# Spare products in TensorE's early pauses, a last result stored in three pieces, and new due times for the first groups of a planned graph-network kernel

## The chip, the core and the metric

The kernel runs on one core of a Trainium2 chip. The metric is the device time of one execution, in microseconds (us). Three runs of the kernel before gave 1441.22, 1442.35 and 1445.91; the median is 1442.35. Engines are called PE (TensorE), DVE (VectorE), ACT (ScalarE), POOL (GpSimd) and SP (SyncE, which here issues nearly all DMAs).

## What is computed

128 graphs of 64 nodes with 256 features pass through four residual layers. Each layer takes a layernorm and a relu of the running x and adds its result to x:

```python
h = jnp.maximum(_layernorm(x), 0.0); x = x + _L0_gnn_ref(h, adj, ...)   # attention, 4 heads of 64, elu
h = jnp.maximum(_layernorm(x), 0.0); x = x + _L1_gnn_ref(h, adj, ...)   # attention, 1 head of 256, elu
h = jnp.maximum(_layernorm(x), 0.0); x = x + _L2_gnn_ref(h, nodemask, adj, ...)  # relations by label, relu
h = jnp.maximum(_layernorm(x), 0.0); x = x + _L3_gnn_ref(h, adj, ...)   # three GRU steps
...
for i in range(3):                       # inside _L3_gnn_ref
    m = h @ weight[i]
    aggr = jnp.einsum('bst,bsd->btd', A, m)
    h = _gru_cell(aggr, h, w_ih, w_hh, b_ih, b_hh)
```

Everything is float32. The adjacency holds only zeros and ones, so of layer 2 only the relation with label 1 has edges. The kernel computes that case in its planned part and holds a general part behind a flag, which these inputs do not take.

## The kernel before, in words

**Tiling.** Two graphs fill 128 partitions; four such pairs are a group (`G = 4`, `T = 512` columns), and there are 16 groups. Each group goes through layers 0, 1 and 2 (`first_layer`, `second_layer`, `third_layer`), then through `before` (layernorm of the GRU's input and its first product along the edges) and `recur`, the three GRU steps. Groups 0 and 1 are split into two units of two pairs, `(p0, n) = (0, 2)` and `(2, 2)`; the second unit of group 0 uses tiles of its own (names ending in `e`, as `t0e`, `hT1e`, `u2e`), so that its work can lie beside that of the first. From group 2 on a group is one unit. Groups 0 and 1 transpose on PE (`layernorm_T`), later ones by 32x32 blocks on DVE and 16 DMAs (`layernorm_T_by_dma`).

**Setting up.** Beside groups 0 and 1 the kernel prepares weights: the columns of the attention vectors (`attention_columns`, on DVE), the loop relation's weights `wl`, and the GRU's weights `wc` and `whh` (`later_weights`, mostly PE products copied out by ACT).

**What orders the work.** The code does not run in program order. Each operation is noted with an estimated cost (`Plan.note`, function `cost`), and `Plan.emit` then acts as a list scheduler: it keeps one planned clock for each engine (`free`), finds for each engine the ready operation that can start first, settles ties by a due time, and emits it. A result is planned to reach another engine `LATENCY` (160.9 ns) after its end. The due times come from jobs opened by `nc.begin(name, start, end, after)`: an operation's due time lies between the job's start and end according to the work still behind it. The stretches of each unit's three layers are the tuples `at` in `units`; from group 3 on they are `end - 55.6 * i`. `start` (99.2) and `period` (83.2) give the due times of the recurrences. The engines then run these fixed orders and wait on semaphores; the plan's times themselves bind nothing on the chip.

**PSUM.** Eight banks: three tagged `mt`, shared by products of all layers, and five owned by the recurrence (`ry`, `rm`, `rz`, `nh`, `ni`). Until the recurrence first takes one of its own, the others may borrow all five (`Banks.place`, `early`).

**The end.** The recurrence works on the features in two chunks of 128. After the last step `back` transposes a chunk on PE and DVE adds the residual x out of PSUM into `hnat`: chunk 0 in the middle of the last step, chunk 1 after it. Then one DMA stores all of `hnat` (512 KB). After that each engine reads the flag and branches past the general part.

In the profile all planned operations carry the line of `emit` (L380) and the packed products of `beside` carry L601, so names of tiles are used here: `hn`, `hT` are a layernorm and its transpose, `t` the attention weights, `u` and `v` layer 2, `st`, `mv`, `var` the layernorm's statistics, `tp` a PSUM bank with transposes, `mm` one with products.

Of the kernel before, what the change touches and what calls it, by code (L numbers as in the profile page):

```python
# [20 lines left out]
G = 4  # L21
# [186 lines left out]
class Plan:  # L208

    LATENCY = 160.9

    def __init__(self, nc):
        self.nc, self.on, self.ops, self.job = nc, False, [], None
        self.jobs = {}
        for name in ENGINES:
            setattr(self, name, Engine(self, name))

# [46 lines left out]
    def emit(self):  # L266
# [45 lines left out]
        while left:  # L312
            best = None
            for e, ops in ready.items():
                found = None
                for op in ops:
                    t = max(free[e], op.ready)
                    if best is not None and t > best[0] or found is not None and t > found[0] and t > free[e]:
                        continue
                    if any(j.left for j in op.job.after):  # L320
                        continue
                    places = {}
                    for b in op.needs:
                        if b.real is None:
                            taken = [tag for x, tag in places.items() if x.pool is b.pool]
                            tag = b.pool.place(b, taken)
                            if tag is None:
                                break
                            places[b] = tag
                            t = max(t, b.pool.released(tag, b, taken.count(tag)))  # L330
                    else:
                        key = (t, op.due)
                        if found is None or key < found[:2]:
                            found = (*key, op, places)
                if found is not None and (best is None or found[:2] < best[:2]):
                    best = found
            assert best is not None, "nothing can be emitted"
            t, _, op, places = best
            e = op.engine
            ready[e].remove(op)  # L340
            for b, tag in places.items():
                b.pool.put(b, tag)
            op.call()
            op.start = t
            if op.dma:
                free[e] = t + 665.0
                wire = max(wire, t + 1350.0) + op.cost
                op.end = wire + 400.0
            else:
                took = op.cost  # L350
                if op.port:
                    other = "Pool" if e == "DVE" else "DVE"
                    took = max(took, held[other] + min(op.port, took) - t)
                    held[e] = t + took
                op.end = t + took + (165.0 if e == "PE" else 0.0)
                free[e] = t + took - min(early.get(e, 0.0), op.cost / 2)
            for b in op.bases:
                b.left -= 1
                b.end = max(b.end, op.end)
            op.job.left -= 1  # L360
            left -= 1
            for other in op.then:
                other.waits -= 1
                if not other.waits:
                    enter(other)
# [71 lines left out]
def kernel(  # L437
# [167 lines left out]
        writes = list({id(x[0].base): x[0] for x in products}.values())  # L605
        nc.note("PE", emit, cost, [Plan.all_of(x) for x in writes], [x for p in products for x in p[1:]])

    def elu_add(work, src, o, engine):

        em = work.tile(list(o.shape), F32, name="em")  # L610
        nc.vector.tensor_scalar(em, o, 0.0, None, op0=ALU.min)
        nc.scalar.activation(em, em, AF.Exp)
        nc.vector.scalar_tensor_tensor(em, em, -1.0, o, op0=ALU.add, op1=ALU.max)
        engine.tensor_tensor(src, src, em, ALU.add)

# [3 lines left out]
            b = slice(half * N, (half + 1) * N)  # L619
            nc.vector.tensor_scalar(dst[b, :, b], src[b], scalar, None, op0=op)  # L620

    def values(work, psum, src, heads, we, by_dma=False, graphs=False):


        fo = D // heads
        n = src.shape[1]
        hT = work.tile([P, K, n * P], F32, name="hT")
        if by_dma:
            layernorm_T_by_dma(work, src, hT, graphs=graphs)
        else:  # L630
            layernorm_T(work, psum, src, hT, graphs=graphs)
        wh = work.tile([P, n, D + heads], F32, name="wh")
        wv = wh.rearrange("p g (h f) -> p g h f", h=heads)
        nc.gpsimd.memset(wv[:, :, :, fo:], 1.0)
        es = work.tile([P, n, 2 * heads], F32, name="es")
        for p in range(n):
            pm = psum.tile([P, 512], F32, name="mm")
            for k in range(K):
                nc.tensor.matmul(
                    pm[:, : D + 2 * heads], pair(hT, k, p) if graphs else hT[:, k, p * P : (p + 1) * P], we[:, k, :],  # L640
                    start=(k == 0), stop=(k == K - 1),
                )
            nc.scalar.copy(wv[:, p, :, :fo], pm[:, :D].rearrange("p (h f) -> p h f", h=heads))
            nc.vector.tensor_copy(es[:, p, :], pm[:, D : D + 2 * heads])
        return wv, es

    def aggregate(work, psum, lhsT, wv, heads):
# [13 lines left out]
            )  # L661
        return o.rearrange("p g h f -> p g (h f)")

    def aggregate_graphs(work, psum, t, wv, heads):


        fo = D // heads
# [2 lines left out]
        for u in range(n // 2):  # L670
# [9 lines left out]
            for r in range(2):  # L680
                rec = work.tile([P, heads], F32, name="rec")
                nc.vector.reciprocal(rec, pv[r][:, :, fo])
                nc.vector.tensor_tensor(
                    o[:, 2 * u + r], pv[r][:, :, :fo], rec[:, :, None].to_broadcast([P, heads, fo]), ALU.mult
                )
        return o.rearrange("p g h f -> p g (h f)")

    def along(psum, hnat, abd, aT, cs):
# [54 lines left out]
            state_sums(aT, aS, k)  # L743
        return hT, aT, hS, aS

    def recurrence(work, psum, start, src, abd, store):

        hT, aT, hS, aS = start

        def back(hT, hnat, c, plus=None):  # L750

            pt = psum.tile([P, G, P], F32, name="tp")
            for p in range(G):
                nc.tensor.transpose(pt[:, p, :], hT[:, c, p * P : (p + 1) * P], ident)
            if plus is None:
                nc.scalar.copy(hnat[:, :, c * P : (c + 1) * P], pt)
            else:
                nc.vector.tensor_tensor(hnat[:, :, c * P : (c + 1) * P], pt, plus[:, :, c * P : (c + 1) * P], ALU.add)
            return 0.45

        class Chunk:

# [88 lines left out]
        for i in range(LAYERS):  # L851
# [71 lines left out]
            if not last:  # L923
                for k in range(K):
                    state_sums(hT, hS, k)
        back(hT, hnat, 1, src)
        store(hnat)

    with ExitStack() as s1:
# [4 lines left out]
        class Banks(Pool):  # L936
# [14 lines left out]
            def place(self, base, taken):  # L951
                if base.tag in self.own:
                    return super().place(base, taken)
                for tag in ("mt", *self.own) if self.early else ("mt",):
                    live = sum(1 for b in self.live.get(tag, ()) if b.left)
                    if live + taken.count(tag) < self.room(tag, base):
                        return tag
# [122 lines left out]
        def attention(g, p0, n, layer, heads, we, pool):  # L1080
# [1 line left out]

            nh = n * heads
            src = XG[g][:, p0 : p0 + n]
            wv, es = values(pool, psum, src, heads, we, g >= AHEAD, True)
            if layer == 0 and p0 == 0:
                MT[g] = edge_bounds(g)
            mt = MT[g][:, p0 : p0 + n]
# [41 lines left out]
            for q in range(0, n, m):  # L1130
# [3 lines left out]
                t4 = t[:, c].rearrange("p (g h) i -> p g h i", g=m)  # L1134
                edges = mt[:, q : q + m, None, :].to_broadcast([P, m, heads, N])
                nc.vector.tensor_tensor(t4, t4, edges, ALU.min)
            o = aggregate_graphs(pool, psum, t, wv, heads)
            elu_add(pool, src, o, nc.vector if g < 1 else nc.gpsimd)

        def first_weights():  # L1140
            attention_columns(w0e, H, (AB[:, 0, :], AB[:, 1, :]))
# [87 lines left out]
        def recur(g):  # L1229
            recurrence(  # L1230
                W[3], psum, START.pop(g), XG[g], ABD[g],
                lambda h: nc.sync.dma_start(outr[:, g * G : (g + 1) * G, :], h),
            )

        nc.begin("columns")
# [1 line left out]
        nc.begin("weights", 18.0, 79.1)  # L1237
        later_weights(early)
        layers = (first_layer, second_layer, third_layer)
        start, period = 99.2, 83.2  # L1240
        users = {}
        for g in range(NG):
            if g > 1:
                load_group(g)

            if g == 0:
                units = [(0, 2, (0.2, 24.7, 61.4, 71.1)), (2, 2, (-0.6, 32.2, 60.6, 75.0))]
            elif g == 1:
                units = [(0, 2, (27.2, 56.6, 87.4, 98.1)), (2, 2, (44.7, 71.4, 101.8, 129.4))]
            elif g == 2:  # L1250
                units = [(0, G, (72.8, 120.6, 177.5, 238.7))]
            else:
                end = start + g * period - 26.2
                units = [(0, G, [end - 55.6 * i for i in (3, 2, 1, 0)])]
            for p0, n, at in units:
                spare = g == 0 and p0 > 0
                for i in range(3):
# [5 lines left out]
                nc.begin("make")  # L1263
                nc.note("-", make_gru, 0.0, [], [], [op for op in nc.ops if any(b.pool is early for b in op.bases)])
            at = start + g * period
            nc.begin(("before", g), at - (13.0 if g == 0 else 21.2), at, [("recur", g - 2)] if g > 1 else [])
            before(g)
            nc.begin(("recur", g), at, at + period)
            recur(g)
# [20 lines left out]
        amr = once.tile([1, 1], F32, name="amr")  # L1290
        nc.vector.tensor_reduce(amr, top2, AX.X, ALU.max)
        nc.vector.tensor_scalar(flag, amr, 2.0, None, op0=ALU.is_ge)
        with tc.manual_schedule(engines={getattr(mybir.EngineType, e) for e in ENGINES.values()}):
            nc.emit()


    def general():
        with ExitStack() as s2:
# [4 lines left out]
            with ExitStack() as s3:  # L1303
# [4 lines left out]
                with tc.For_i(0, NP, G) as p0:  # L1308
                    xs, at = fetched(work, X, p0)
                    start = before_recurrence(work, psum, xs, at, abd)  # L1310
                    recurrence(
                        work, psum, start, xs, abd, lambda h: nc.sync.dma_start(outr[:, bass.ds(p0, G), :], h)
                    )

    def fetched(pool, rows, p0):
# [194 lines left out]
```

## Time and profile before

| what | value |
|---|---|
| median of 3 runs | 1442.35 us |
| the profiled execution's own time | 1441.89 us |
| its span, first to last instruction | 1440.1 us |
| PE busy in the span | 1387.4 us (96%), 9461 instructions |
| DVE busy | 1044.3 us (73%) |
| ACT busy | 779.0 us (54%) |
| POOL busy | 596.5 us (41%) |
| mean granted PE clock | 0.990 |
| chain that ended last, by engine | PE 80%, DVE 7%, SP's queue 5% |

One way to read such a page: PE is busy nearly all the time, so what counts is where it is not, and whether it then runs at its full clock. The view by windows answers both. It gives for each stretch the busy time and the number of instructions of each engine (the count in brackets), the clock that PE was granted (1.00 is full), the DMA engines' share and GB/s. A float32 product shows as two PE instructions, a transpose as one. The chain of waits gives, for the chain of work that ended last, what it consisted of at each time: start, duration, engine and tile; "issue" is time in which nothing that the profile shows was waited for.

### The profile page before, as it was taken

How to read it: one execution, taken by the hardware profiler on the slowest of the kernel's cores; microseconds unless marked ns; L12 is line 12 of the kernel's file. 1: busy time of each engine (PE TensorE's matmuls, PEld its weight loads, DVE VectorE, ACT ScalarE, POOL GpSimd, SP SyncE). 2: the span in 40 equal slices, each digit the busy share in tenths (PEclk: the TensorE clock that was granted, in tenths of full speed). 3: DMA queues.
4: the chain of work that ended last, by engine and by line, in shares of the span. 5: the costliest groups of instructions: out<-in, count | busy, mean ns of one | idle time of the engine just before them, and what ended most of it. 6: DMA issues, size and time to landing. Idle time of an engine off the chain costs nothing.

```text
span 1440.1 us, 27350 instructions
## 1 busy us (share of the span) xinstructions
PE 1387.4 (96%) x9461; PEld 942.8 (65%) x9461; DVE 1044.3 (73%) x2743; ACT 779.0 (54%) x1853; POOL 596.5 (41%) x744
## 2 busy tenths in 40 slices
PE   4989999999999999999999999999999999999997
PEld 3655676666767666666766666676767666666664
DVE  6569588686968878696886869687776968664544
ACT  3655556555565555555555555556555555554543
POOL 1524524433434453443444344344444434352432
PEclk8999999999999999999999999999999999999998
DMA  7010221122223122222312222231212122111000
GB/s 212 19 27 19 42 60 32 37 57 53 62 44 72 32 46 57 48 60 47 72 31 51 52 46 60 50 70 30 60 30 38 45 46 55 23 26 23 16 15 18
DMA packets 298873, 67.85 MB, mean 47 GB/s; under 512 B 274664, under 2 KB 296936, under 8 KB 298728
## 3 DMA queue, kind: packets, MB, share of 16 engines
q1 hardware_dynamic: 298168, 65.50, 21.6%
q8 instruction: 78, 1.28, 0.4%
q14 instruction: 67, 0.55, 0.1%
q10 hardware_dynamic: 560, 0.52, 0.1%
HBM read 28.06 MB, written 8.53 MB: 25 GB/s over the span
## 4 chain that ended last, share of the span: by engine, by line
PE 80%; DVE 7%; SPq 5%; ACT 3%; issue 2%; DMA 2%; POOL 1%; DVEq 0%; POOLq 0%; ACTq 0%
PE ry L380 21%; PE mm L380 15%; PE ni L380 10%; PE rz L380 10%; PE nh L380 10%; PE rm L380 5%; SPq L380 5%; PE tp L380 4%; PE mm L601 3%; PE tp L601 3%; DVE t L380 1%; ACT hn L380 1%; DVE d L380 1%; DMA t<-row 1%; DVE hn L380 1%
## 5 line engine op out<-in xcount | busy, mean ns | idle before, releaser
L380 POOL TENSOR_TENSOR d<-hT,t 128x256 f32<-128x256 f32 x192 | 149.7, 790 | 456.1 <-ACT t L380 454.2
L380 PE MATMUL ni<-aT,wc 128*128 128x512 f32 x384 | 195.1, 596 | 1.2 <-DVE t L380 1.2
L380 PE MATMUL nh<-hT,whh 128*128 128x512 f32 x384 | 194.0, 597 | 0.4 <-ACT t L380 0.3
L380 ACT ACTIVATE z<-z,brz 128x256 f32<-128x256 f32 x192 | 97.1, 506 | 117.2 <-DVE z L380 116.7
L380 ACT COPY z<-ry 128x256 f32<-128x256 f32 x192 | 70.8, 369 | 157.0 <-PE ry L380 99.8
L380 DVE SCALAR_TENSOR_TENSOR t<-r,t 128x256 f32<-128x256 f32 x192 | 107.3, 563 | 63.7 <-ACT r L380 53.2
L380 POOL TENSOR_TENSOR hS<-hT 128x256 f32<-128x256 f32 x96 | 78.3, 819 | 154.9 <-PE ry L380 124.8
L380 DVE SCALAR_TENSOR_TENSOR d<-z,d 128x256 f32<-128x256 f32 x192 | 109.6, 580 | 29.1 <-POOL d L380 19.0
L380 PE MATMUL ry<-hS,wsum 128*128 128x256 f32 x384 | 116.3, 385 | 3.0 <-ACT z L380 3.0
L380 PE MATMUL rz<-hS,whh 128*128 128x256 f32 x384 | 117.6, 388 | 1.4 <-DVE z L380 1.4
L380 PE MATMUL mm<-wl,hT 128*128 128x512 f32 x248 | 117.8, 598 | 0.0
L380 ACT ACTIVATE hn<-xg,var,rstd 128x256 f32<-128x256 f32 x200 | 109.2, 594 | 13.7 <-DVE var L380 12.0
L380 PE MATMUL rz<-aS,wc 128*128 128x256 f32 x384 | 114.5, 380 | 0.0
L380 PE MATMUL ry<-aS,wsum 128*128 128x256 f32 x384 | 114.3, 379 | 0.0
L380 ACT ACTIVATE t<-t,bi 128x256 f32<-128x256 f32 x192 | 93.6, 502 | 35.9 <-DVE t L380 35.4
L380 DVE TENSOR_TENSOR z<-rz,z 128x256 f32<-128x256 f32 x192 | 80.0, 416 | 42.2 <-PE rz L380 24.1
L380 PEld LDWEIGHTS ry<-hS,wsum 128*128 128x128 f32 x384 | 70.0, 190 | 47.3 <-issue 24.9
L380 DVE SCALAR_TENSOR_TENSOR hT<-d,t 128x256 f32<-128x256 f32 x192 | 97.7, 521 | 3.7 <-ACT wh L380 0.2
L380 POOL TENSOR_TENSOR rstd<-var,mhalf 128x4 f32<-128x4 f32 (+1 forms) x70 | 68.2, 975 | 75.4 <-DVE var L380 73.8
L380 DVE BATCH_NORM_STATS2 st<-xg 128x6 f32<-128x256 f32 x256 | 96.6, 411 | 3.0 <-DMA xg<-in_x_dram 3.0
L380 POOL TENSOR_TENSOR hS<-hT,hS 128x256 f32<-128x256 f32 x96 | 73.4, 765 | 46.3 <-DVE hT L380 44.2
L380 PEld LDWEIGHTS ni<-aT,wc 128*128 128x128 f32 x384 | 71.6, 190 | 24.1 <-issue 10.6
(200 smaller groups left out, 3162.4 us busy)
## 6 DMA issues: line engine op xcount, KB each, us to landing
hT<-hn SPq DMA_DIRECT2D x896, 32.0 KB, 1.9
out_dram<-hnat SPq DMA_DIRECT2D x16, 512.0 KB, 3.1
xg<-in_x_dram SPq DMA_DIRECT2D x15, 512.0 KB, 4.6
t<-row SPq DMA_DIRECT2D x28, 256.0 KB, 3.7
at<-in_adj_dram SPq DMA_DIRECT2D x64, 32.0 KB, 2.2
eg<-in_adj_dram SPq DMA_DIRECT2D x64, 32.0 KB, 2.1
ag<-in_adj_dram SPq DMA_DIRECT2D x16, 128.0 KB, 2.4
t<-row SPq DMA_DIRECT2D x28, 64.0 KB, 2.6
```

The source lines that it names most:

```text
L380: return do(*[real(a) for a in args], **{k: real(v) for k, v in kwargs.items()})
L601: nc.nc.tensor.matmul(*[real(x) for x in product], start=True, stop=True)
```

## The change

Four things change together.

1. **Spare products.** A tile `warm` of 128x128 ones is set on DVE, as its first instruction. `emit` puts products `warm` x `warm` into PE's order wherever PE's planned pause before an operation is at least 320 ns and the operation is planned before 115 us: one per 220 ns, after a first 100 ns. They write the PSUM bank `ni`, and nothing reads it. The bank is therefore no longer lent out early (four of the five own banks are).
2. **Last result in three pieces.** In the last group `back` stores what it has added: chunk 0 (256 KB) when it is there, then chunk 1 in two halves of two pairs (128 KB each). The two halves also split the last transposes and the last addition.
3. **Due times.** `start` 99.2 to 93.6, `period` 83.2 to 83.8, the tuples of groups 0, 1 and 2, the spacing of later groups (55.6 to 53.5), the lead of `before` (21.2 to 22.3), and `LATENCY` (160.9 to 164.2).
4. **Branches not taken.** `by_scalar` would move some work of DVE to ACT, but it is passed as `g < 0`, which no group fulfils.

```diff
-    LATENCY = 160.9
+    LATENCY = 164.2
...
             ready[e].remove(op)
+            if e == "PE" and self.spare and t < 115.0 * 1e3:
+                for _ in range(int((t - free[e] - 100.0) / 220.0)):
+                    self.spare()
...
-    def recurrence(work, psum, start, src, abd, store):
+    def recurrence(work, psum, start, src, abd, store, in_parts=False):
...
+                nc.vector.tensor_tensor(hnat[part], pt, plus[part], ALU.add)
+                if in_parts:
+                    store(hnat, part)
...
-        back(hT, hnat, 1, src)
-        store(hnat)
+        if in_parts:
+            for p0 in (G // 2, 0):
+                back(hT, hnat, 1, src, p0, G // 2)
+        else:
+            back(hT, hnat, 1, src)
+            store(hnat, slice(None))
...
-                for tag in ("mt", *self.own) if self.early else ("mt",):
+                for tag in ("mt", *self.own[: 4 if 115.0 else 5]) if self.early else ("mt",):
...
-        start, period = 99.2, 83.2
+        start, period = 93.6, 83.8
...
-                units = [(0, 2, (0.2, 24.7, 61.4, 71.1)), (2, 2, (-0.6, 32.2, 60.6, 75.0))]
+                units = [(0, 2, (-2.5, 24.3, 61.4, 71.1)), (2, 2, (-2.7, 25.3, 58.8, 74.4))]
...
-                units = [(0, 2, (27.2, 56.6, 87.4, 98.1)), (2, 2, (44.7, 71.4, 101.8, 129.4))]
+                units = [(0, 2, (27.5, 54.4, 87.5, 95.7)), (2, 2, (45.3, 71.4, 100.6, 129.4))]
...
-                units = [(0, G, (72.8, 120.6, 177.5, 238.7))]
+                units = [(0, G, (72.8, 119.1, 176.7, 238.7))]
...
-                units = [(0, G, [end - 55.6 * i for i in (3, 2, 1, 0)])]
+                units = [(0, G, [end - 53.5 * i + x for i, x in ((3, 0.0), (2, 0.0), (1, 0.0), (0, 0.0))])]
...
-            nc.begin(("before", g), at - (13.0 if g == 0 else 21.2), at, [("recur", g - 2)] if g > 1 else [])
+            nc.begin(("before", g), at - (13.0 if g == 0 else 22.3), at, [("recur", g - 2)] if g > 1 else [])
...
+        if 115.0:
+            warm = const.tile([P, P], F32, name="warm")
+            nc.nc.vector.memset(warm, 1.0)
+            pause = psum.real.tile([P, P], F32, name="ni", tag="ni", bufs=1)
+            nc.spare = lambda: nc.nc.tensor.matmul(pause, warm, warm, start=True, stop=True)
```

In the built program the scheduler has placed 159 spare products in 22 places: 38 before the first transpose, 14 before the first product with `w0e`, then 1, 2, 5, 18 and 25 up to the second layer's first transposes, 23 in 10 places in the stretch with the weights, and 7, 12, 8, 5 and 1 around the third layer of group 0. In the same program the second unit of group 0 is put ahead: its layer-1 products with `w1e` now come before the transposes of `ihn`, and its weights `t1e` before group 1's `t0`. But for these, the added `memset` and the split of the last pieces, the counts of work on all engines are the same.

More of the change, by code (lines that the diff above doesn't have):

```diff
@@ L216, in __init__ @@
         self.jobs = {}
+        self.spare = None
         for name in ENGINES:
@@ L606, in beside, with elu_add @@
         nc.note("PE", emit, cost, [Plan.all_of(x) for x in writes], [x for p in products for x in p[1:]])
-    def elu_add(work, src, o, engine):
+    def elu_add(work, src, o, engine, by_scalar=False):
         em = work.tile(list(o.shape), F32, name="em")
-        nc.vector.tensor_scalar(em, o, 0.0, None, op0=ALU.min)
-        nc.scalar.activation(em, em, AF.Exp)
+        if by_scalar:
+            nc.scalar.activation(em, o, AF.Relu, scale=-1.0)
+            nc.scalar.activation(em, em, AF.Exp, scale=-1.0)
+        else:
+            nc.vector.tensor_scalar(em, o, 0.0, None, op0=ALU.min)
+            nc.scalar.activation(em, em, AF.Exp)
         nc.vector.scalar_tensor_tensor(em, em, -1.0, o, op0=ALU.add, op1=ALU.max)
@@ L620, in block_diagonal, with values @@
             nc.vector.tensor_scalar(dst[b, :, b], src[b], scalar, None, op0=op)
-    def values(work, psum, src, heads, we, by_dma=False, graphs=False):
+    def values(work, psum, src, heads, we, by_dma=False, graphs=False, by_scalar=False):
         fo = D // heads
@@ L643, in values @@
             nc.scalar.copy(wv[:, p, :, :fo], pm[:, :D].rearrange("p (h f) -> p h f", h=heads))
-            nc.vector.tensor_copy(es[:, p, :], pm[:, D : D + 2 * heads])
+            (nc.scalar.copy if by_scalar else nc.vector.tensor_copy)(es[:, p, :], pm[:, D : D + 2 * heads])
         return wv, es
@@ L662, in aggregate, with aggregate_graphs @@
         return o.rearrange("p g h f -> p g (h f)")
-    def aggregate_graphs(work, psum, t, wv, heads):
+    def aggregate_graphs(work, psum, t, wv, heads, by_scalar=False):
         fo = D // heads
@@ L682, in aggregate_graphs @@
                 nc.vector.reciprocal(rec, pv[r][:, :, fo])
-                nc.vector.tensor_tensor(
-                    o[:, 2 * u + r], pv[r][:, :, :fo], rec[:, :, None].to_broadcast([P, heads, fo]), ALU.mult
-                )
+                if heads == 1 and by_scalar:
+                    nc.scalar.activation(o[:, 2 * u + r, 0], pv[r][:, 0, :fo], AF.Identity, scale=rec[:, 0:1])
+                else:
+                    nc.vector.tensor_tensor(
+                        o[:, 2 * u + r], pv[r][:, :, :fo], rec[:, :, None].to_broadcast([P, heads, fo]), ALU.mult
+                    )
         return o.rearrange("p g h f -> p g (h f)")
@@ L744, in before_recurrence, with back @@
         return hT, aT, hS, aS
-    def recurrence(work, psum, start, src, abd, store):
+    def recurrence(work, psum, start, src, abd, store, in_parts=False):
         hT, aT, hS, aS = start
[L750 to L754, printed above, removed]
+        def back(hT, hnat, c, plus=None, p0=0, n=G):
+            pt = psum.tile([P, n, P], F32, name="tp")
+            for p in range(n):
+                nc.tensor.transpose(pt[:, p, :], hT[:, c, (p0 + p) * P : (p0 + p + 1) * P], ident)
+            part = (slice(None), slice(p0, p0 + n), slice(c * P, (c + 1) * P))
             if plus is None:
-                nc.scalar.copy(hnat[:, :, c * P : (c + 1) * P], pt)
+                nc.scalar.copy(hnat[part], pt)
             else:
-                nc.vector.tensor_tensor(hnat[:, :, c * P : (c + 1) * P], pt, plus[:, :, c * P : (c + 1) * P], ALU.add)
-            return 0.45
+                nc.vector.tensor_tensor(hnat[part], pt, plus[part], ALU.add)
+                if in_parts:
+                    store(hnat, part)
         class Chunk:
@@ L925, in recurrence @@
                     state_sums(hT, hS, k)
-        back(hT, hnat, 1, src)
-        store(hnat)
+        if in_parts:
+            for p0 in (G // 2, 0):
+                back(hT, hnat, 1, src, p0, G // 2)
+        else:
+            back(hT, hnat, 1, src)
+            store(hnat, slice(None))
     with ExitStack() as s1:
@@ L1084, in attention @@
             src = XG[g][:, p0 : p0 + n]
-            wv, es = values(pool, psum, src, heads, we, g >= AHEAD, True)
+            wv, es = values(pool, psum, src, heads, we, g >= AHEAD, True, g < 0)
             if layer == 0 and p0 == 0:
@@ L1136, in attention @@
                 nc.vector.tensor_tensor(t4, t4, edges, ALU.min)
-            o = aggregate_graphs(pool, psum, t, wv, heads)
-            elu_add(pool, src, o, nc.vector if g < 1 else nc.gpsimd)
+            o = aggregate_graphs(pool, psum, t, wv, heads, g < 0)
+            elu_add(pool, src, o, nc.vector if g < 1 else nc.gpsimd, g < 0)
         def first_weights():
@@ L1231, in recur @@
                 W[3], psum, START.pop(g), XG[g], ABD[g],
-                lambda h: nc.sync.dma_start(outr[:, g * G : (g + 1) * G, :], h),
+                lambda h, part: nc.sync.dma_start(outr[:, g * G : (g + 1) * G, :][part], h[part]),
+                g == NG - 1,
             )
@@ L1311, in general @@
                     recurrence(
-                        work, psum, start, xs, abd, lambda h: nc.sync.dma_start(outr[:, bass.ds(p0, G), :], h)
+                        work, psum, start, xs, abd, lambda h, _: nc.sync.dma_start(outr[:, bass.ds(p0, G), :], h)
                     )
```

## The prediction

> **What bounds the kernel now.** I read the page's slices first: PE is full from the fourth slice on, and the clock digit is below 9 only at the two ends.
>
> ```profile
> PE   4989999999999999999999999999999999999997
> DVE  6569588686968878696886869687776968664544
> PEclk8999999999999999999999999999999999999998
> ```
>
> So the pauses that the spare products can reach are in the first 115 us. The view by windows shows them (busy PE, PEld, DVE, ACT, POOL with counts, then clock):
>
> ```profile
> 25.00:30.00 5.00, 2.31 (x11) 2.21 (x11) 4.93 (x15) 0.63 (x1) 0.97 (x1) 0.50 0.66 134
> 30.00:35.00 5.00, 0.55 (x6) 0.17 (x4) 5.00 (x22) 1.30 (x3) 1.48 (x4) 0.50 0.75 212
> 35.00:40.00 5.00, 4.68 (x16) 3.49 (x17) 2.01 (x12) 4.88 (x12) 3.18 (x5) 0.63 0.20 56
> 80.00:85.00 5.00, 5.00 (x16) 1.98 (x17) 5.00 (x20) 0.67 (x3) 2.35 (x3) 1.00 0.00 0
> 85.00:90.00 5.00, 3.79 (x22) 1.41 (x20) 4.94 (x15) 3.23 (x8) 0.00 (x0) 1.00 0.12 26
> 90.00:95.00 5.00, 1.74 (x9) 0.41 (x8) 4.96 (x22) 1.01 (x3) 2.67 (x4) 0.83 0.33 54
> 95.00:100.00 5.00, 4.26 (x13) 3.16 (x14) 1.26 (x8) 4.83 (x11) 1.05 (x2) 0.50 0.29 47
> ```
>
> Twice DVE is full while PE starves, and twice PE then starts its next full stretch at half clock. Over 0 to 100 us PE idles 26.9 us; over all the rest 25.8, of which 6.8 lie behind its last instruction. Which of these pauses sets the time is told by the chain of waits (start, duration, what):
>
> ```profile
> 9.17 1.46 issue
> 10.63 2.98 PE mm L380 x6
> ...
> 17.89 0.53 ACT t0e L380
> 18.44 0.90 DVE t0e L380
> ...
> 33.70 1.09 ACT hn L380 x2
> 34.79 0.49 ACT whh L380
> 35.28 0.04 issue
> 35.32 2.82 PE tp L380 x12
> ...
> 79.08 0.64 ACT hn L380
> 79.75 0.69 DVE hn L380
> ...
> 95.87 0.60 ACT hn L380
> ```
>
> It runs over PE to 18 us, DVE to 33.7, PE (with ACT's copies) from 35.3 to 79, DVE to 95.8, then PE nearly to the end. PE's idle time inside the DVE stretches is hidden; its clock at their ends is not. From 100 on the useful work is fixed, so the end moves with the time at which PE becomes full, with later stalls, and with the tail.
>
> **Spare products, price of one.** It is two passes of 128 columns. Passes of 128 columns start 109 ns apart in the transposes at 41 us and 213 ns apart at 28 us, at half clock: 0.22 us warm, 0.43 cold. 159 are 34.7 us warm, more than the 26.9 us that PE idles there.
>
> **The first 52.** The engines start at 0.8 us and `warm` is there at about 1.1. In the trace a cold PE speeds up 3.3 to 4.5 us after work begins (35.3 to 38.65, 95.4 to 99.95, and 10.6 to 14.7: passes of 264 columns fall from 440 to 223 ns there, though the clock column reads 1.00). Some 9 products run cold (3.9 us), 29 warm (6.3): the first transposes move from 7.35 to about 11.3. They take 0.44 instead of 1.4; 14 more (3.05) put the first `w0e` product at 14.9 instead of 10.63, 4.3 later. It then runs warm: six passes, four transposes and two passes that took 4.5 us take 2.2, and DVE, idle 10.7 to 13.65, has done `top`, `m`, `amax` in that gap. Then `m`'s transposes, a spare and eight passes (2.2) to 19.4, the product with `same` (0.86 + 0.16) and ACT's 0.6 put `t0e` at about 21.1 instead of 18.44: **2.7 us late**, 1.5 if the clock rises early. The 8 between there and the first packed products lie in PE's waits; the 18 end at 28.0, before DVE wants the second packed result (26.9, late by 2.7: 29.6); the 25 end near 34.
>
> **Where that delay goes.** DVE's list is full until 33.7, so it comes 2.7 late, but the new order asks for the second unit's `var` before `w1e`'s reduction, `xg` and the statistics (0.60 + 0.60 + 1.2 on DVE), so its `hn` on ACT still starts at about 33.6. PE resumes at 34.2, warm, and does the unit's transposes and `w1e` products (0.44 + 1.74) with the 12 of `hhn` (1.3). At 38.65 before had done 2.2 us (warm) of this stage's list; after has done 2.4. **Net 0**; without the moved-up `var` it would be +2.
>
> **Covered.** The `memset` (0.17) lies in DVE's idle time before 4.49. SP now issues the four `at` loads (4.33) ahead of `ihn`, which is wanted at 35.3, over 20 us after it lands. One bank less to lend can hold a product until ACT has emptied one (copies take 0.37 to 0.6); no row shows a bank wait apart, the ends are 0 and +2, and I take 0, since even with five banks the stretch from 35.3 to 79 shows only 1.6 us of open gaps, from all causes together.
>
> **35 to 79 us.** 23 spare products are 5.0 us; the same stretch of before has 2.8 us of open gaps, 1.2 of them before 35.3. They were placed against the planned pauses of the new order, of which I can check only that waits of 0.4 to 0.7 us before `ihT` products exist in before (0.26 and 0.56 shown as idle). Bounds: 0 if all lie in real waits, +3.4 if only 1.6 does. Since ACT now puts an exponential (0.63) ahead of the `gT` copy at the longest of them, I take **+1.1**.
>
> **79 to 106 us.** DVE's list from `es0` to the last `var` is nearly the same in both orders, only `u2` now waits for `wl` products that stand behind one of the second unit; it stays full for 16.1 us. If it starts at 79.1 + 1.1, with the earlier exponential on ACT (-1.1), PE again gets `hn` at 95.4. The 33 spares there (7.2 us) fill the 4.9 us of gaps and what the moved products leave. Then PE is warm: 95.4 to 99.95 held 4.5 us of busy PE at half clock, **-2.2**, and 0.5 of transposes waiting on ACT is overlapped. [...] 25 to 38.65 and 93.65 to 100 are 20 us[...]. The rows say less: PE was busy only 6.2 and 4.9 us of these, 5.5 lost, and of that 1.7 + 2.2 on the chain. I use the rows. [...] here the column falls at 25.0, 0.7 after PE's last work, behind 5 us with 2.0 busy[...].
>
> Sum to here: 0 + 1.1 - 2.2 - 0.8 (the overlap, and transposes of `before` moved behind its first edge products) = **-1.9**, bounds -5.5 (the second unit's lead, 35 to 79 at 0, DVE 2 earlier) and +4.
>
> **Due times and LATENCY.** Between 115 and 365 us before has 5.4 us of PE gaps above 0.1 us (1.47 at 297.7 before packed products that wait for DVE's `t`, 0.70 at 176, 0.50 at 142), in the groups whose tuples move. From 365 to 1365 the period of 83.23 is full but for 7.5 us of single stalls (0.64 at 682, 1.9 at 1050, 1.7 at 1220, 3.0 from 1282 to 1340). The order alone does not show which go; one 0.89 at 1308.7 does, since two `wl` products now stand in it. Bounds -7 and +4 (the plan can open new ones). I take half of the first groups' gaps, **-2.7**.
>
> **Last pieces.** The rows at the end:
>
> ```profile
> 1432.62 0.69 PE L380 MATMUL tp<-ident,hT 128*128 128x128 f32 x2 [0.18 <-DVE hT L380]
> 1433.35 0.69 DVE L380 TENSOR_TENSOR hnat<-tp,xg 128x512 f32<-128x512 f32 x1 [0.79 <-PE tp L380]
> 1434.06 0.38 SPq L380 DMA_DIRECT2D out_dram<-hnat  x1
> ```
>
> The last addition halves to 0.42 (the row of `z`, 128x256 from PSUM, is 0.416): -0.27. The DMA lands 3.1 us after issue with 512 KB, about 2.2 to 2.4 with 128 (the rows of `eg` and `ag`). But SP branches at 1434.49, and its next record is at 1438.19, 0.9 after that landing: the branch, not the DMA, is last there. So **-0.3**, -1.2 if the landing were. The two further issues (0.4 each) stand on SP ahead of the last and end before 1433.8; nothing else is queued behind them.
>
> **Sum.** -1.9 - 2.7 - 0.3 = -4.9 on the profiled 1441.89, 1437.0; the median of the runs lies 0.46 above that execution: **1437.4**.
>
> **Rivals.** (a) The pauses are shorter on the chip than in the plan, and the spares overrun them: the first 52 hand 2.7 through DVE's full list (the moved `var` then helps nothing, since DVE's later work is late all the same), the 23 add 3.4, the last 33 add 7.2 - 4.9 = 2.3. Less the half clock on the chain (1.7 + 2.2) and 0.3 that is 4.2 late: 1446.5, slower. It decides if the first `w0e` product starts after 15 us and PE reaches the `ihn` transposes after 41. (b) The new stretches carry: layer 2 of group 0 gets through sooner, as PE's bare sum of passes from 38.65 on would allow (3.5 in all), and two thirds of the 13 us of stalls go: -3.5 - 8.5 - 0.3, 1430. For it: `start` is set 5.6 us earlier; against: DVE's full list from 80 to 96. (c) Nothing much: the 2.2 is spent again from 35 to 79, old stalls go and new ones come; 0.3 of the tail and some 0.5 are left: 1441.5.
>
> **Chances.** Within 0.3% (4.3 us) is about what a measurement of this kernel can tell from no change. The forecast's own case (1433 to 1440.5) 0.57, (b) 0.18, (c) 0.19, (a) 0.06. Faster by over 0.3% means below 1438.0: (b) and some 0.41 of the forecast's case, 0.59; slower 0.05; same 0.36. The range of 8 in 10 takes in most of (b) and (c): 1430 to 1443.
>
> **What would show it.** PE's clock 1.00 in every window from 20 to 115; the first `w0e` product at 14 to 15.5; `t0e` on DVE at 20 to 22; `ihn` transposes at 38 to 40; the first packed products along the edges (106.4 before) at 103 to 106; PE gaps from 115 to 365 near 3 us; a last addition of 0.42. If PE is full earlier than 100, (b) is right; if `hn` comes at 97 or later, (a) or (c). A period other than 83.2 between groups 4 and 10 would make all of it wrong.

## The result, and the profile after

| kernel | median | of runs |
|---|---|---|
| before | 1442.39 us | 4 (1441.22 to 1445.91) |
| after | 1434.66 us | 4 (1434.47 to 1435.02) |

The ratio is 0.9942, with a 95% interval of 0.9926 to 0.9958: about 8 us faster. The forecast was 1437.4 (1430 to 1443), so it has the sign, and the time lies inside the range. That it came so near is in part luck: as the experiments below show, the sum behind it was too good for the first 106 us and too small for what follows. The profiled execution took 1434.47, its span 1432.45.

The page's slices of after, the same three rows as shown of before:

```profile
PE   9999999999999999999999999999999999999997
DVE  5568688686867878686887868688686868774544
PEclk9999999999999999999999999999999999999999
```

PE is now full from the first slice on, and its clock digit is 9 throughout. The view by windows says the same for the stretches in which PE starved (PE, PEld, DVE, ACT, POOL, clock):

```profile
25.00:30.00 5.00, 5.00 (x71) 4.81 (x71) 4.14 (x14) 0.63 (x1) 0.00 (x0) 1.00 0.60 147
...
35.00:40.00 5.00, 5.00 (x41) 4.45 (x39) 4.18 (x27) 3.58 (x8) 1.76 (x3) 1.00 0.09 19
...
95.00:100.00 5.00, 5.00 (x47) 4.37 (x47) 3.85 (x21) 2.71 (x7) 2.97 (x5) 1.00 0.31 51
```

It is tempting to stop here: clock at 1.00, PE at 5.00 of 5.00, 8 us gained. But busy now counts the spares, so these rows no longer tell whether useful work is sooner. The chain of waits does (start, duration, what):

```profile
1.06 10.84 PE ni L1315 x76
11.90 0.44 PE tp L384 x4
12.34 3.13 PE ni L1315 x28
15.46 0.89 PE mm L384 x4
...
20.85 0.61 ACT t0e L384
21.48 0.70 DVE t0e L384
...
106.30 0.20 PE tp L605 x2
```

and of before, at the same place:

```profile
106.40 0.20 PE tp L601 x2
```

The chain of the first 15 us is the spares themselves (`ni`, 38 and 14 products). `t0e` on DVE starts at 21.48 instead of 18.44, and the first packed products along the edges at 106.30, where before had 106.40. So the whole prefix, with its full clock, came out even, and not quite that: by a count of PE's order, eight transposes, one `w0e` product and one of `ry` (0.87 + 0.44 + 0.43 = 1.7 us) now stand behind the edges. With the same work done, after is thus 1.6 us later there. All that was gained lies behind it. PE's gaps over 0.02 us, summed from the trace's PE rows, fell from 5.5 to 1.8 us between 115 and 365 us and from 8.0 to 4.4 between 365 and 1365, and the end is shorter:

```profile
1425.88 0.69 PE L384 MATMUL tp<-ident,hT 128*128 128x128 f32 x2 [0.43 <-DVE hT L384]
1426.19 1.24 SPq L384 DMA_DIRECT2D out_dram<-hnat  x2
1426.61 0.42 DVE L384 TENSOR_TENSOR hnat<-tp,xg 128x256 f32<-128x256 f32 x1 [0.44 <-PE tp L384]
```

The last addition is 0.42 instead of 0.69, and from the end of the last `hT` to the end of the span it is 6.6 us instead of 7.6.

### The profile page after: what moved, and what is told of

Its sections match the earlier page's. It is cut to its first block, busy times and chain, and to the rows that moved or that the text cites. A ratio compares the mean times of both kernels' runs of the same rounds, so it can differ in the third digit from the quotient of the medians.

```text
span 1432.5 us, 28063 instructions
## 1 busy us (share of the span) xinstructions
PE 1412.5 (99%) x9779; PEld 973.6 (68%) x9779; DVE 1041.5 (73%) x2745; ACT 778.7 (54%) x1853; POOL 597.7 (42%) x744
## 4 chain that ended last, share of the span: by engine, by line
PE 88%; DVE 4%; SPq 3%; ACT 3%; DMA 1%; issue 1%; POOL 1%; DVEq 0%; POOLq 0%; ACTq 0%
PE ry L384 22%; PE mm L384 16%; PE rz L384 11%; PE ni L384 11%; PE nh L384 10%; PE rm L384 5%; PE tp L384 4%; PE mm L605 3%; SPq L384 3%; PE tp L605 2%; PE ni L1315 2%; DVE d L384 1%; POOL d L384 1%; DVE hT L384 1%; DMA t<-row 1%
## 5 line engine op out<-in xcount | busy, mean ns | idle before, releaser
L384 DVE SCALAR_TENSOR_TENSOR d<-z,d 128x256 f32<-128x256 f32 x192 | 127.2, 669 | 58.1 <-POOL d L384 45.2
L384 POOL TENSOR_TENSOR hS<-hT 128x256 f32<-128x256 f32 x96 | 73.9, 770 | 175.5 <-PE ry L384 136.3
L384 DVE SCALAR_TENSOR_TENSOR t<-r,t 128x256 f32<-128x256 f32 x192 | 98.0, 511 | 50.2 <-ACT r L384 44.5
L384 DVE TENSOR_TENSOR z<-rz,z 128x256 f32<-128x256 f32 x192 | 80.2, 418 | 59.1 <-PE rz L384 46.6
L384 DVE BATCH_NORM_STATS2 st<-xg 128x6 f32<-128x256 f32 x256 | 98.5, 413 | 3.2 <-DMA xg<-in_x_dram 2.5
L384 DVE SCALAR_TENSOR_TENSOR hT<-d,t 128x256 f32<-128x256 f32 x192 | 91.9, 485 | 6.1
L384 PEld LDWEIGHTS nh<-hT,whh 128*128 128x128 f32 x384 | 70.1, 190 | 27.3 <-issue 17.4
L384 PEld LDWEIGHTS ry<-aS,wsum 128*128 128x128 f32 x384 | 73.0, 190 | 22.7 <-issue 10.3
```

The lines of the kernel that those rows point to most:

```text
L384: return do(*[real(a) for a in args], **{k: real(v) for k, v in kwargs.items()})
```

## The experiments

Each kernel is compared with the kernel before on the same chip. Milestones of the traces, in us from the span's start ("edges" are the first packed products along the edges; the gaps are PE's, as above). Each row is one execution; that of `spares_first` took 1437.51, 2.5 over its median, that of `no_spares` 1430.18, 1.2 under:

| kernel | first `w0e` | `t0e` on DVE | last early `var` | edges | gaps 115-365, 365-1365 | span |
|---|---|---|---|---|---|---|
| before | 10.63 | 18.44 | 95.71 | 106.33 | 5.5, 8.0 | 1440.1 |
| after | 15.30 | 21.48 | 98.50 | 106.23 | 1.8, 4.4 | 1432.5 |
| no_spares | 10.17 | 17.99 | 95.20 | 103.32 | 1.4, 3.8 | 1428.1 |
| spares_first | 15.64 | 21.82 | 100.26 | 109.08 | 2.0, 4.3 | 1435.5 |
| spares_late | 10.31 | 18.27 | 95.29 | 103.13 | 2.1, 3.7 | 1428.9 |
| spares_fit | 10.55 | 16.80 | 93.81 | 101.55 | 1.9, 3.9 | 1427.2 |

The `var` is the last that layer 2 of group 0 needs from DVE's full list. The gap sums of one trace are good to about 1 us: before and `pieces_only` have the same order of PE but for the last pieces and 13.5 and 12.9 us in all, the five kernels in the new order 5.3 to 6.3.

### The four parts, one by one

**Without spares (`no_spares`).** The changed kernel, the order of all other work untouched:

```diff
-            if e == "PE" and self.spare and t < 115.0 * 1e3:
+            if e == "PE" and self.spare and t < 0.0 * 1e3:
```

> The changed kernel with its spare products left out and nothing else moved (same order on every engine; the bank stays unlent and the ones tile is still set). Theory A, the gain comes from fewer stalls of PE after 115 us (7.6 us less gaps by the traces) and from the tail (about 0.9), and the spare products are worth nothing net, since what they cost ahead of 40 us and between 79 and 99 us eats what the warm clock brings: 1433.5 to 1436.5, and the first packed edge products near 106 with clock drops back at 25 and 95 us. Rival B, the warm clock is what pays (rows: 1.7 and 2.2 us on the chain): 1437.5 to 1440. Below 1433.5 would mean that the spares cost time.

1431.35 us, ratio 0.9924 [0.9910, 0.9938]. That is below what either theory expected: the spares cost time. Its chain:

```profile
10.17 2.10 PE mm L384 x4
...
17.36 0.61 ACT t0e L384
17.99 0.70 DVE t0e L384
...
103.39 0.20 PE tp L605 x2
```

`t0e` on DVE starts at 17.99, 3.5 us sooner than in after, and the edges at 103.39 are 2.9 sooner than after's 106.30, with the half clock back at 25 and 95 us:

```profile
25.00:30.00 5.00, 0.00 (x0) 0.00 (x0) 4.97 (x16) 0.63 (x1) 1.13 (x2) 0.50 0.52 149
...
95.00:100.00 5.00, 4.52 (x17) 3.52 (x18) 1.14 (x8) 4.51 (x11) 1.01 (x1) 0.66 0.26 47
```

**Spares alone (`spares_only`).** The kernel before with the spares and the bank kept for them; old numbers, one store.

```diff
+            if e == "PE" and self.spare and t < 115.0 * 1e3:
+                for _ in range(int((t - free[e] - 100.0) / 220.0)):
+                    self.spare()
...
-                for tag in ("mt", *self.own) if self.early else ("mt",):
+                for tag in ("mt", *self.own[: 4 if 115.0 else 5]) if self.early else ("mt",):
```

> The kernel before with the spare products (and the bank kept for them), old due times, one store. Theory A: 1441.4 to 1443.5, the same as before. Rival B: 1437.5 to 1440.5, the half clock at 35.3 and 95.4 us gone and nothing given back. If the spares overrun the pauses: 1444 to 1447.

1445.46, ratio 1.0021 [1.0013, 1.0028]: slower by 3 us. `t0e` on DVE at 21.21, edges at 108.96. Both kernels give the spares as placed the same price, +2.6 to +3 us (here with the bank that they take, which leaves PE's order of tiles as it was).

**Due times alone (`due_only`).** All new numbers and LATENCY in the kernel before; no spares, five banks lent, one store.

```diff
-    LATENCY = 160.9
+    LATENCY = 164.2
...
-        start, period = 99.2, 83.2
+        start, period = 93.6, 83.8
...
-                units = [(0, 2, (0.2, 24.7, 61.4, 71.1)), (2, 2, (-0.6, 32.2, 60.6, 75.0))]
+                units = [(0, 2, (-2.5, 24.3, 61.4, 71.1)), (2, 2, (-2.7, 25.3, 58.8, 74.4))]
...
```

The other lines are those of the change from its `g == 1` to the lead of `before`.

> The kernel before with the new due times and LATENCY alone (no spares, five banks lent, one store). Theory A: 1434.5 to 1437.5, gaps of PE from 115 us on some 7 us less than before. Rival B: 1439 to 1441 (the 2.7 that the prediction gave to the due times, or less).

1435.58, ratio 0.9950 [0.9937, 0.9964], as theory A expected. Gaps 2.6 and 2.9 us, edges at 104.33. But the order has moved more here: 24 passes (4.7 us) that before does ahead of the edges stand behind them, so with the same work done the edges would be at 109.0, 2.7 us later than in before.

**Pieces alone (`pieces_only`).** The kernel before with the stores in three pieces.

```diff
-        back(hT, hnat, 1, src)
-        store(hnat)
+        if in_parts:
+            for p0 in (G // 2, 0):
+                back(hT, hnat, 1, src, p0, G // 2)
```

> The kernel before with the three last pieces alone. If SP's last branch is independent of the store (prediction): -0.3, 1442.1. If it ends with the landing of the last DMA (traces: 7.57 us from the last hT to the end before, 6.63 after): -0.9, 1441.5.

1441.72, ratio 0.9992 [0.9983, 1.0001]: -1.2 us, but the interval holds both 0 and 2.4, so the time doesn't decide. Over all traces here, the stretch from the last `hT` to the end is 7.3 to 7.9 us in the seven kernels with one store and 6.0 to 7.1 in the seven with three, 7.5 and 6.8 in the mean: some 0.7 to 0.8. The last addition is 0.27 of that; the rest is SP's and varies by over a us between kernels with the same last instructions.

Due times (-7.2), spares (+3.0) and pieces (-1.2) sum to -5.4, not to the -8.4 of the whole. What remains separates `due_only` from `no_spares` too (0.9950 to 0.9924, 3.7 us): three pieces, the `memset`, and one bank fewer to lend early, which alters PE's order within the first 224 us. The traces show where it lies: with the work moved behind them counted (1.7 and 4.7 us), the edges are at 105.1 in `no_spares` and 109.0 in `due_only`. The pieces leave PE's order ahead of the edges as it was, and the `memset` is no part of the plan, so these 3.9 us come from the order made with one bank fewer. That holds for this set of numbers: with the old ones (`spares_only`) the same bank changes nothing in the order. It wasn't tried by itself, and each ratio has an interval of 2 us to either side.

### Which of the spares cost

**First 52 dropped (`spares_late`), first 52 alone (`spares_first`), first two batches sized (`spares_fit`).** `counts` replaces the planned number of the first places:

```diff
+        self.counts = [0, 0]                  # spares_late
+        self.counts = [38, 14] + [0] * 100    # spares_first
+        self.counts = [18, 9]                 # spares_fit
...
+                n = int((t - free[e] - 100.0) / 220.0)
+                if n > 0 and self.counts:
+                    n = self.counts.pop(0)
```

> The changed kernel without the first two batches of spare products (38 and 14, ahead of 15 us); the other 107 stay. Theory C: the 52 of the start hold PE's real work up by 3 us and DVE hands that on to the end, the later ones lie in real pauses: the w0e product back near 10.2, and 1429 to 1431.5 (without any spares 1431.35; up to 2 us better by the warm clock at 31 and 95 us). Rival D: it is the 56 spares from 41 to 100 us (12 us of PE) that cost: 1433.5 to 1435, like the changed kernel.

1431.40, ratio 0.9923 [0.9909, 0.9936]: theory C, and the same as without any. Yet the clock is 1.00 here from 25 to 35 and from 95 to 100 us. So the full clock there brought nothing that the time shows.

> The changed kernel with the first 52 spares alone. Theory C: 1434 to 1436, first packed edge products near 106 to 107. Rival D: 1431 to 1432.5, as without spares.

1434.99, ratio 0.9937 [0.9923, 0.9951], again theory C: these 52 alone bring the changed kernel's time. (The 109.08 for the edges is of the slow execution named above.)

> The changed kernel with 18 and 9 spares in the first two batches, sized to PE's measured pauses there (6.2 us before the first transposes, with 9 of the 18 cold at 0.43; 1.8 to 2.4 before the w0e product), the other 107 as they are. Theory C: the w0e product at 10.2 to 10.8, then six passes, transposes and ten more passes warm, so t0e on ACT up to 2 us sooner than 17.4: 1427.5 to 1430. If the warm clock at the start is worth nothing (ACT or DVE last there): as spares_late, 1429 to 1431.5. Rival D: 1433.5 to 1435.

1428.74, ratio 0.9898 [0.9883, 0.9913]: on one chip, 27 sized spares at the start gain 2.7 us on none (`spares_late`), where the 52 planned ones (`spares_first`, without the later ones) lose 3.6. The trace says where. The `w0e` products start at 10.55, 0.2 to 0.4 later than without, but warm: the first four passes take 1.13 us, where `no_spares` took 2.10, and `t0e` on DVE follows at 16.80 instead of 18.27.

```profile
10.55 1.13 PE L388 MATMUL mm<-w0e,hT0e 128*128 128x264 f32 x4
...
16.17 0.60 ACT L388 ACTIVATE t0e<-mm 128x512 f32<-128x512 f32 x1
16.80 0.69 DVE L388 TENSOR_TENSOR t0e<-t0e,gd0e 128x512 f32<-128x512 f32 x1 [1.32 <-ACT t0e L388]
```

These 1.5 us reach the edges (101.55 for 103.13) and the end of the profiled executions (1427.2 for 1428.9); the remaining 1 us of the medians lies within the spread of the runs.

**Sized spares in the old order (`before_fit`).** `spares_only` with the same two counts.

> The kernel before with spare products whose first two batches are sized to the measured pauses (18 and 9 for 38 and 13), the others as the plan places them. With unsized batches it was 1.0021 of before. Theory C (the start's batches hold up real work, warm passes from 10 us on bring 1.5 to 2.5): 1439.5 to 1442.5 where before is 1443. If the overrun of the later batches costs in this order: 1443 to 1446.

1439.83, ratio 0.9980 [0.9971, 0.9989], where the planned counts gave 1.0021. So the sign of the spares is set by these two batches in both orders.

### Which of the numbers

**All but the tuples of groups 0 to 2 (`no_new_tuples`).** `LATENCY`, `start`, `period`, lead and spacing new, tuples old; otherwise the kernel before.

```diff
-                units = [(0, G, [end - 55.6 * i for i in (3, 2, 1, 0)])]
+                units = [(0, G, [end - 53.5 * i + x for i, x in ((3, 0.0), (2, 0.0), (1, 0.0), (0, 0.0))])]
...
-            nc.begin(("before", g), at - (13.0 if g == 0 else 21.2), at, [("recur", g - 2)] if g > 1 else [])
+            nc.begin(("before", g), at - (13.0 if g == 0 else 22.3), at, [("recur", g - 2)] if g > 1 else [])
```

with the two lines of `LATENCY` and `start, period` as above.

> The kernel before with LATENCY, start, period, the lead of the step ahead of the recurrence and the later groups' spacing as changed, but with the old tuples of groups 0 to 2. If the stalls that went between 115 and 365 us and the 2 us ahead of the first packed edge products belong to the tuples: 1438.5 to 1441, with the single stalls from 365 on some 4 us less. If the whole gain is the later groups' spacing: 1435 to 1437, as all due times together.

1432.98, ratio 0.9927 [0.9913, 0.9940]: better than with the tuples, though the intervals touch, and outside both forecasts. Gaps 0.6 and 3.3 us. The stalls between 115 and 365 us went without the tuples that were set for those groups.

**LATENCY alone (`latency_only`); the rest without it (`spacing_only`).** The first has one line changed, the second the other lines of `no_new_tuples`.

```diff
-    LATENCY = 160.9     # latency_only
+    LATENCY = 164.2
```

> The kernel before with LATENCY 164.2 instead of 160.9 and nothing else. All later numbers of the plan together give 0.9927 of before. Theory E, the gain is made by the wider stretches of groups from 3 on (spacing, lead, start, period): 1441 to 1445, the same within 0.2%. Theory F, any new set of numbers makes the list scheduler find another order and this one is merely good: anything from 1434 to 1448, gaps from 115 us on that differ from before in place and sum (5.5 + 8.0 us in before).

1483.83, ratio 1.0279 [1.0264, 1.0295]: 41 us slower, for 3.3 ns in a constant. Even theory F had not allowed for that.

> The kernel before with start 93.6, period 83.8, the lead of 22.3 and the spacing 53.5 as changed, but LATENCY 160.9 and the old tuples of groups 0 to 2. Theory E: 1432 to 1436, with less than 5 us of gaps from 115 to 1365 us. Theory F: anywhere up to 1444.

1444.22, ratio 1.0010 [1.0003, 1.0016]: theory E falls. Gaps 2.3 and 11.3. Neither half of the numbers gains; together they give -10 us. The scheduler turns each set into some order, and the order repeats from group to group. PE's rows of one group in `latency_only`, the last column the idle time and who ended it:

```profile
562.59 0.70 PE L384 MATMUL rz<-hS,whh 128*128 128x256 f32 x2 [0.52 <-DVE z L384]
563.13 0.59 PE L384 MATMUL rz<-aS,wc 128*128 128x256 f32 x2
565.10 0.70 PE L384 MATMUL ry<-hS,wsum 128*128 128x256 f32 x2 [1.38 <-ACT z L384]
565.64 0.59 PE L384 MATMUL ry<-aS,wsum 128*128 128x256 f32 x2
566.70 0.70 PE L384 MATMUL ry<-hT,wsum 128*128 128x256 f32 x2 [0.46 <-ACT z L384]
```

The recurrence's products follow each other with no other group's work between them, so PE waits three times for ACT and DVE, 2.4 us. The wait of 1.38 stands in each of ten groups from 304 to 1093 us, with the 0.46 behind it in nine. The period is 86.5 us there at best instead of 83.2, and more in some groups, with what the last section shows. The nine periods together are 39.8 us longer than at 83.2, nearly all of the 41.

### The best of both

**`best`.** Old tuples, the other new numbers, three pieces, sized spares (18 and 9, later 17, 25 and 20 for 19, 29 and 27).

> Old tuples of groups 0 to 2, all other new numbers, three pieces, and spares sized to measured pauses (18 and 9 at the start, 17, 25 and 20 for 19, 29 and 27 later, the rest as planned). From the ratios: 0.9927 by the numbers alone, 0.9974 by sized spares against none in the changed kernel, 0.9992 by the pieces: 0.989 to 0.990, 1427 to 1430. If sized spares only help in the changed order: 0.9915 to 0.993, 1431 to 1433.

1430.72, ratio 0.9914 [0.9900, 0.9928]. Better than both kernels, but behind the number expected, and not distinguishable from `spares_fit` (0.9898). It has the fewest gaps of all from 115 us on (0.3 and 3.3), and its edges at 100.95, but 4.7 us of before's work stand behind these, 1.7 in `spares_fit`. With the same work done its edges are at 105.6 and those of `spares_fit` at 103.3: it is 2.3 us behind there and has 2.2 fewer gaps afterwards, so the two come out even.

## Why the prediction was right, and where it was not

**Price of a spare, and the first 52: right.** 38 took 10.84 us (forecast about 10.2): by the spacing of its passes, 0.213 and then 0.111, 10 were cold, not 9; 14 took 3.13 (3.05). The first `w0e` product came at 15.3 (14.9), `t0e` on DVE at 21.48 (21.1), 3.0 late.

**"Net 0" at 38.65: the step that failed.** The moved-up `var` did what was said: `hn` on ACT, 33.6 in the forecast, is at 33.62. But it was used as the cover for the spares' delay, and it would have been there without them: in `no_spares` the same `hn` is at 30.13. So the delay was not absorbed, it was only set off against a gain of another part. It then went through DVE's list in full: 3.5 us at `t0e`, 3.3 at the last early `var` (95.20 against 98.50), 2.9 at the edges. From `t0e` to that `var` it is 77.0 us in after, `spares_late` and `spares_fit`, and 77.2 in `no_spares`, so what happens ahead of `t0e` is handed on nearly as it is. The second cover was PE's full clock from 35 to 38.65 us (1.7 of half clock on the chain). It brought 0.2 at most: with the half clock the stretch takes 77.2 in `no_spares` and 77.3 in before, with the full one 77.0 in `spares_late` and 77.3 in `before_fit`. A delay that DVE hands on is the first mechanism of rival (a), at 3 us. Its two conditions were half met (the first `w0e` product after 15 us, but `ihn` at 39.1, not after 41), since they too were measured from before, where the order's own gain hid the delay. The forecast's sign for (a) or (c), `hn` at 97 or later, did come: PE starts its transposes at 98.5.

**35 to 79 us, +1.1, and the list behind it.** DVE's list began at 81.46 (`es`), not at 80.2, and took 17.0 us, not 16.1: it waits 0.70 and 0.17 for the `wl` products of `u`. `no_spares` takes the same 17.0 (78.17 to 95.20), so that is the order's doing and not the spares'. PE was foreseen to start the transposes of `hn` at 95.4.

**Warm clock at 95 us, -2.2: too large.** From the last early `var` to the edges it is 8.1 us in `no_spares` and 7.8 in `spares_late`, in the same order; 10.6 in before and 9.7 in `before_fit`, in the old one. The two other pairs that differ in the clock there give 1.1 (8.8 in `spares_first`, 7.7 in after) and 0.2 (10.6 in before, 10.4 in `spares_only`). The clock's price there is 0.2 to 1.1 us. The trace of `no_spares` shows why:

```profile
94.90 0.33 PE L384 MATMUL tp<-ident,hn 128*128 128x128 f32 x1 [1.53 <-ACT hn L384]
95.39 1.11 PE L384 MATMUL tp<-ident,hn 128*128 128x128 f32 x4 [0.16 <-ACT hn L384]
96.83 0.90 PE L384 MATMUL tp<-ident,hn 128*128 128x128 f32 x3 [0.32 <-ACT hn L384]
```

Five of the eight cold transposes lie ahead of a wait for ACT's next `hn`; a faster PE would only have waited longer there. The forecast charged every busy us at half clock, those ahead of that wait of 0.32 us too. What the clock did pay for lies at 10 to 18 us, where PE is most of the chain: from the first `w0e` product to `t0e` it is 6.2 us in after and 6.3 in `spares_fit`, 7.8 in before and `no_spares`. The forecast had these 1.6 us too (4.3 late at the product, 2.7 at `t0e`), but as a discount on the delay of the first 52. Only with the start sized do they remain as a gain.

**The prefix, -1.9: it was -0.1**, as 2.9 of spares against 3.0 of the new order (106.33 to 103.32 without them). Of the 3.0, 1.7 is the work that only moved behind the edges; the forecast had put that and an overlap at 0.8. Without the spares the new order is 1.3 us ahead at the edges with the same work done, with them 1.6 behind.

**One bank fewer, 0:** -3 to -4 with the new numbers, by what remains when the other parts are taken off; not tried by itself.

**Due times and LATENCY, -2.7: they were -7.2** in `due_only`, and all of it behind the edges: its gaps from 115 us on are 8.0 us less than before's, and 2.7 of that are lost ahead of the edges. The gaps from 115 to 365 fell by 3.7 in the changed kernel (forecast 2.7, "near 3 us" left, 1.8 measured). The 3.6 that went from 365 on were left at 0 because the order alone didn't show them. This is the second half of rival (b) (8.5 of stalls gone, measured 7.3 in the changed kernel). Of its first half, 3.5 us by a sooner layer 2, the 1.3 just named were there at most, and they went into the spares' price. The forecast also looked for this gain "in the groups whose tuples move". It came without those tuples. With them the kernel before was some 3 us slower (0.9950 against 0.9927, intervals that touch); `best` and `spares_fit` show no such loss.

**Last pieces, -0.3:** some -0.7 to -0.8, with the addition at 0.42 as foreseen; so SP's end moves too, and is not as independent of the store as the one trace of before suggested; what it waits for stays open.

So -4.9 stood for a measured -7.7 (medians): the prefix came out 1.8 worse than forecast, what lies behind it 4.6 better, and the error is the difference.

## What to carry to other kernels

Work that is put into planned pauses must be sized by the pauses that the trace shows, above all at the start, where PE is the chain: 27 spares there gained 1.5 to 2.7 us and 52 lost about 3. When two edits move the same milestone, compare with the kernel that has one of them; against the kernel before, a gain can look like cover. And a milestone compares two orders only where the same work lies ahead of it. Where a list scheduler makes the order, a number of the plan has no effect of its own: measure whole sets, and look in the trace for a wait that repeats in every group.

## What the hardware showed that was not expected

The same short stalls are sometimes followed by half clock and sometimes not. In `latency_only` the three waits above occur in each group; at 562 to 567 the clock stays at 1.00, one group later, with the same three waits (0.52, 1.39 and 0.46), it falls. The view by windows:

```profile
560.00:565.00 5.00, 3.21 (x22) 1.75 (x13) 4.06 (x10) 1.78 (x3) 0.67 (x1) 1.00 0.25 41
565.00:570.00 5.00, 4.44 (x19) 3.07 (x20) 5.00 (x11) 2.42 (x7) 2.59 (x3) 1.00 0.01 3
...
650.00:655.00 5.00, 3.15 (x8) 1.84 (x7) 4.84 (x8) 1.60 (x4) 3.25 (x3) 0.68 0.07 12
655.00:660.00 5.00, 5.00 (x15) 3.44 (x15) 3.44 (x15) 2.19 (x6) 1.00 (x2) 0.64 0.00 0
```

Five microseconds with some 3.2 of busy PE, in waits of at most 1.4, stand ahead of a fall in one case and not in the other. In the same trace the ten waits of 1.38 go as follows:

| wait of 1.38 ends | clock that follows | to the end of the next such wait |
|---|---|---|
| 304.72 | 1.00 | 86.54 us |
| 391.26 | 1.00 | 87.28 us |
| 478.54 | 1.00 | 86.56 us |
| 565.10 | 1.00 | 86.61 us |
| 651.71 | 0.50 | 90.13 us |
| 741.84 | 0.50 | 88.08 us |
| 829.92 | 1.00 | 86.54 us |
| 916.46 | 0.50 | 88.72 us |
| 1005.18 | 0.50 | 88.11 us |
| 1093.29 | 1.00 | - |

The clock fell in four of the ten groups, and the length of the stall does not tell which; what decides it was not shown. In the group at 650 us, the two `ry` products after the stall take 1.17 and 1.06 us instead of 0.70 and 0.59, and of the nine periods in that trace the five in which the clock stays are 86.5 to 87.3 us, the four in which it falls 88.1 to 90.1.
